# A two-layer megakernel: pair sums on TensorE with a 513th column, and a rearranged hand-over between its layers

## The chip, the cores and the metric

The kernel runs on one core of one Trainium2 chip. The metric is device time in microseconds (us), the median of several executions. Beside the timed executions there is one profiled execution, whose records make up the trace: which instruction ran when on which engine, and what it waited for. The engines are PE (TensorE matmul; PEld is its weight load), DVE (VectorE), ACT (ScalarE), POOL (GpSimd, which also issues the indirect DMAs) and SP (SyncE, which issues most other DMAs). PSUM is the memory that PE writes, in banks of 128x512 f32; SBUF is the working memory that all engines read.

## The reference

Eight sequences of 512 tokens with 128 channels go through two layers. In each the input x is layer-normed (xn), a mixer gives s, a mixture of experts gives g, and x becomes x + s * silu(g).

- Layer 0's mixer is a Mamba block (a recurrent scan over 16 states) with a small MLP; its experts are 24, of which each token uses two, in two rounds with a layer norm between them.
- Layer 1's mixer is causal attention with 8 heads over tokens scaled to unit length; its experts are 128, two per token.

What the change touches is, in the reference's words:

```python
# layer 0, per group of tokens; dispatch and combine pick two experts per token
h = moe_apply(xf, combine, dispatch, W1, b1)          # [tokens, 512], a weighted sum of two experts' rows
h = relu(layer_norm(h, lw, lb))
out = moe_apply(h, combine, dispatch, W2, b2)         # again a sum of two rows per token
g = silu(layer_norm(out + xn, ln_out_w, ln_out_b))
x = x + s * g
# layer 1
xn = (x - m) / sqrt(v + 1e-5)
l2 = sqrt(sum(xn * xn));  xa = xn / max(l2, 1e-12) * sqrt(128) * gamma    # attention's input
logits = xn @ wg                                                          # the router's input
```

## The kernel before

All of it is one program for one core. Python code lists the instructions; a planner then orders each engine's list by place in the program and an own model of costs, within the dependencies, so that an engine's order can differ from the program's (on DVE, a later pair's line 539 runs ahead of an earlier pair's line 553). On the chip each engine takes its list strictly in order and waits on semaphores. Tiles come from pools: a tag with `bufs=n` has n buffers, and the next use of a buffer waits for the last reader of the one before.

The scan of layer 0 (`model`, 64 steps of two states each) is cut into steps and dealt out beside the other work: 31 steps beside layer 0's experts, and the rest in the hand-over and beside layer 1's first six batches of attention. A step of `scan` takes, for each half of the channels, one multiply on DVE (line 655, 128x1024), two scans (657, 128x512), one multiply (658), and PE transposes that add the result up in PSUM (679). It holds `u`, a tile with four buffers, until 679 has read it.

The stages, with the tiles that matter:

- **First expert round** (`expert1`, 24 times). POOL gathers token rows, PE transposes and multiplies them with the expert's weights into `ph` (lines 503 and 504; tag "pe", four PSUM banks), ACT scales the result by each slot's routing weight into `hs` (505), and SP stores `hs` to `hs_dram`, rows of 512 floats (`store`, lines 474 and 475).
- **Hidden layer norm** (`between`, 16 pairs of token tiles). For each tile POOL gathers the two expert rows of 128 tokens into `hd` (128; four buffers, three pairs ahead). DVE adds the two rows and takes their sum along (539), which line 543 turns into minus the mean. ACT squares with that bias and sums (545), takes the root (549); DVE inverts it (550), applies mean and weight (553), then deviation and bias (554); SP stores to `hid_dram` (556). In four of the pairs `fold` also prepares attention weights on PE, from the same four banks.
- **Second expert round** (`expert2`), from `hid_dram` to `os_dram`.
- **Hand-over**, per batch of 512 tokens. `fetch` loads xn into `o` and gathers onto it, with adding DMAs, the two expert rows of each token (131, eight gathers). `after` layer-norms `o` on DVE (107 to 117) and makes the gate: weight, bias, SiLU, times s, plus x (595 to 599), the SiLU on ACT and the four others on POOL. `prepare` layer-norms the new x to `xn2`, transposes it, multiplies with the router's weights (811), picks the top two (816, 817), then takes the squares' sums on ACT (826), inverts their roots, scales and transposes to `xaT`, attention's input (836), and last calls `route`, which counts slots per expert on PE and DVE and scatters the token rows by POOL (880).
- **Attention beside the scan** (`early`, batches 0 to 5): per head, line 898 and 906 (scores), 908 (mask and maximum on DVE), 912 (exponential), 926 (transposes), 933 (values), 944 (sum). In each batch's heads the next batch is fetched (at head 1), gated (head 3) and prepared (head 4). PSUM for preparing, router and values is the scan's tag "pm" of two banks.
- **End**: attention of batches 6 and 7 beside layer 1's experts, and the final gathers (`finish`).

Of the kernel before, what the change touches and what calls it, by code (L numbers as in the profile page):

```python
# [47 lines left out]
def tile_kernel(ctx: ExitStack, tc: tile.TileContext, t: dict, out: bass.AP):  # L48
# [39 lines left out]
    hs_dram = dram.tile([E0 * SLOTS, DH], F32, name="hs_dram")  # L88
# [25 lines left out]
    def layernorm(pool, src, dst, n, eps, tag):  # L114
        mv, rs = norm_stats(pool, src, n, eps, tag)
        for j in range(n):
            V.tensor_scalar(dst[:, j, :], src[:, j, :], mv[:, j, 0:1], rs[:, j : j + 1], ALU.subtract, ALU.mult)

# [78 lines left out]
    zero = inv_pool.tile([P, L], F32, name="zero")  # L197
    G.memset(zero, 0.0)
# [8 lines left out]

    lg = mb.tile([P, NTT, E0], F32, name="lg", tag="yz")
# [281 lines left out]
    def expert1(e, w):  # L490

        we = w(e)
        px = ps_e.tile([P, SLOTS], F32, name="px", tag="pe")
        for c, r in enumerate(SROWS):
            xg = mg.tile([CP, D], F32, name="xg", bufs=8)
            gather(xg[:r], xn_dram, inv[:r, c, e : e + 1])
            T.transpose(px[:, c * CP : c * CP + r], xg[:r], ident[:r, :r])  # L497
        xT = mg.tile([P, SLOTS], F32, name="xTe", tag="xTe", bufs=2)
        S.copy(xT, px)
        hs = me.tile([CP, SG, DH], F32, name="hs", tag="big", bufs=4)  # L500
        for c, r in enumerate(SROWS):
            ph = ps_e.tile([CP, DH], F32, name="ph", tag="pe")
            T.matmul(ph[:r], chosen(e, r), bias[:, 0:DH], start=True, stop=False)
            T.matmul(ph[:r], xT[:, c * CP : c * CP + r], we, start=False, stop=True)  # L504
            S.activation(hs[:r, c, :], ph[:r], AF.Copy, scale=wsl[:r, c, e : e + 1])
        store(hs_dram, e, hs)

    def between():
# [6 lines left out]
        def begin(h, b0):  # L515
# [6 lines left out]
            hd = me.tile([P, n, 2, DH], F32, name="hd", tag="big", bufs=4)  # L522
# [7 lines left out]
        for i, (h, b0) in enumerate(pairs):  # L530
# [6 lines left out]
            var = st.tile([P, n], F32, name="lnh_v")  # L537
            for j in range(n):
                V.scalar_tensor_tensor(
                    hd[:, j, 0, :], hd[:, j, 0, :], 1.0, hd[:, j, 1, :], ALU.mult, ALU.add,  # L540
                    accum_out=mean[:, j : j + 1],
                )
            V.tensor_scalar(mean, mean, -1.0 / DH, None, ALU.mult)
            for j in range(n):
                S.activation(
                    hd[:, j, 1, :], hd[:, j, 0, :], AF.Square, bias=mean[:, j : j + 1],
                    accum_out=var[:, j : j + 1],
                )
            S.activation(var, var, AF.Sqrt, bias=eps6, scale=1.0 / DH)
            V.reciprocal(var, var)  # L550
            for j in range(n):
                x = hd[:, j, 0, :]
                V.scalar_tensor_tensor(x, x, mean[:, j : j + 1], lw, ALU.add, ALU.mult)
# [23 lines left out]
    def fetch(b):  # L577
# [7 lines left out]
        for h in range(H0):  # L585
            g = h * B + b
            gather_add(o[:, h, :], os_dram, row[:, g, 0:1])
        for h in range(H0):
            gather_add(o[:, h, :], os_dram, row[:, h * B + b, 1:2])
        return o, sb, xb  # L590

    def after(b, o, sb, xb):

        layernorm(st, o, o, NJ, eps6, "lno")
        G.tensor_tensor(o, o, bc(lno_w.unsqueeze(1), (P, NJ, D)), ALU.mult)
        G.tensor_tensor(o, o, bc(lno_b.unsqueeze(1), (P, NJ, D)), ALU.add)
        S.activation(o, o, AF.Silu)
        G.tensor_tensor(o, o, sb, ALU.mult)
        G.tensor_tensor(xb, o, xb, ALU.add)
        Q.dma_start(rows(x1_dram[b][:, :]), xb)  # L600
        return xb
# [190 lines left out]
    class Attention:  # L792


        def __init__(self, at, m_qk, w_vo, ps_x, ps_q, ps_s, ps_t, ps_o):
            self.at, self.m_qk, self.w_vo = at, m_qk, w_vo
            self.ps_x, self.ps_q, self.ps_s, self.ps_t, self.ps_o = ps_x, ps_q, ps_s, ps_t, ps_o

        def prepare(self, b, xb):
# [3 lines left out]
            layernorm(st, xb, xn2, NJ, eps5, "ln1")  # L803
# [18 lines left out]

            sq = at.tile([P, NJ, D], F32, name="sq2", bufs=1)
            ss = st.tile([P, NJ], F32, name="ss2")
            for j in range(NJ):
                S.activation(sq[:, j, :], xn2[:, j, :], AF.Square, accum_out=ss[:, j : j + 1])
            V.tensor_scalar(ss, ss, 1e-24, None, ALU.max)
            S.activation(ss, ss, AF.Sqrt)
            V.reciprocal(ss, ss)
            V.tensor_scalar(ss, ss, float(D) ** 0.5, None, ALU.mult)  # L830
            V.tensor_tensor(sq, xn2, bc(ss.unsqueeze(2), (P, NJ, D)), ALU.mult)
            pt = ps_x.tile([P, L], F32, name="pt3", tag=px)
            for j in range(NJ):
                T.transpose(pt[:, j * P : (j + 1) * P], sq[:, j, :], ident)
            xaT = at.tile([P, L], F32, name="xaT", bufs=3)
            S.activation(xaT, pt, AF.Copy, scale=gamma)
            self.route(b, xn2)
            return xaT
# [302 lines left out]
    def early():  # L1141
        for b in range(EARLY):
            for hd, _ in enumerate(beside.heads(b, ready[b])):
                if hd == 1:
                    got = fetch(b + 1)
                if hd == 3:
                    xb = after(b + 1, *got)
                if hd == 4:
                    ready[b + 1] = beside.prepare(b + 1, xb)
                yield  # L1150
# [28 lines left out]
    for b in range(EARLY + 1, B):  # L1179
        ready[b] = last.prepare(b, after(b, *fetch(b)))  # L1180
    weights2()
# [92 lines left out]
```

## Time and profile before

| | us |
|---|---|
| median of the 3 timed runs | 1579.48 (1574.91 to 1584.55) |
| the profiled execution, its own time | 1590.3 |
| its span (first to last record) | 1588.6 |
| busy: PE / DVE / ACT / POOL | 1213.1 / 1246.7 / 978.7 / 601.3 |
| mean granted TensorE clock | 0.896 |

The page's second part cuts the span into 40 slices of 39.7 us; a digit is the busy share in tenths. "PEclk" is the clock that the throttle granted to PE, in tenths of full speed; the last line is what the DMA engines moved.

```profile
PE   6878798213479888447878989989889798899863
DVE  5687667788846857869999999999899996465454
POOL 1166652656155433673412560042250402010465
PEclk9689999566689999867989999999999999999987
GB/s 181 183 225 261 253 216 253 234 244 245 117 219 226 218 188 154 145 60 107 62 85 68 93 114 48 58 103 73 61 68 61 92 35 14 143 108 235 62 101 96
```

The dip of PE at the seventh to tenth slice is the hidden layer norm, the dip at the seventeenth and eighteenth the hand-over; from there to the 33rd DVE is at 9.

How the views are read: a group of instructions shows its count, its busy time, the mean duration in ns, and the time its engine stood idle just before it with what ended that. The chain of waits is followed back from the last instruction to what released each step. A stretch's row gives the busy time of each engine in it.

### The profile page before, as it was taken

The numbers are of one execution on the slowest core, as the hardware profiler recorded it, in microseconds if no ns is written. First come the engines' busy times: TensorE is split into PE (matmuls) and PEld (weight loads), VectorE is DVE, ScalarE is ACT, GpSimd is POOL, SyncE is SP. The second block draws the span as 40 slices with busy tenths as digits, with TensorE's granted clock in tenths as the row PEclk, the third lists the DMA queues.
The fourth block names the chain that finished last, engine by engine and source line by source line (L and its number), as shares of the span: only waits on it lengthen the run. The fifth ranks groups of instructions, "written<-read, shape, count | busy, mean of one in ns | idle before, by whom it ended". The sixth has DMA issues, their size and how long they took to land.

```text
span 1588.6 us, 20612 instructions
## 1 busy us (share of the span) xinstructions
PE 1213.1 (76%) x6793; PEld 853.8 (54%) x6793; DVE 1246.7 (78%) x2783; ACT 978.7 (62%) x1728; POOL 601.3 (38%) x505
## 2 busy tenths in 40 slices
PE   6878798213479888447878989989889798899863
PEld 4534364113367777434556656766657576567542
DVE  5687667788846857869999999999899996465454
ACT  5356776575648677455767758667586674643442
POOL 1166652656155433673412560042250402010465
PEclk9689999566689999867989999999999999999987
DMA  6578767777377764523222341133121210538233
GB/s 181 183 225 261 253 216 253 234 244 245 117 219 226 218 188 154 145 60 107 62 85 68 93 114 48 58 103 73 61 68 61 92 35 14 143 108 235 62 101 96
DMA packets 170669, 218.84 MB, mean 138 GB/s; under 512 B 16618, under 2 KB 118074, under 8 KB 170562
## 3 DMA queue, kind: packets, MB, share of 16 engines
q1 hardware_dynamic: 126018, 99.39, 20.4%
q10 hardware_dynamic: 18432, 67.12, 13.0%
q0 software_dynamic: 26112, 51.01, 12.4%
q8 instruction: 54, 0.88, 0.2%
q14 instruction: 53, 0.43, 0.1%
HBM read 161.56 MB, written 55.84 MB: 137 GB/s over the span
## 4 chain that ended last, share of the span: by engine, by line
DVE 37%; PE 31%; DMA 8%; issue 8%; ACT 7%; POOL 6%; another core or an unknown queue 1%; SPq 1%; POOLq 0%; DVEq 0%; ACTq 0%
DVE u L657 10%; DVE u L658 4%; PE po L933 4%; PE sc L906 4%; DVE u L655 4%; DVE sc L908 3%; POOL o L131 3%; PE py L679 3%; PE pp L926 2%; PE po L573 2%; PE pc L611 2%; DVE s L944 2%; DMA hd<-hs_dram,row 2%; PE ph L504 2%; PE pv L891 1%
## 5 line engine op out<-in xcount | busy, mean ns | idle before, releaser
L657 DVE TENSOR_TENSOR_SCAN u<-da,u 128x512 f32<-128x512 f32 x256 | 312.6, 1243 | 64.1 <-ACT da L653 47.5
L679 PE MATMUL py<-ident,u 128*128 128x128 f32 x1024 | 164.3, 301 | 138.8 <-DVE u L658 137.3
L679 PEld LDWEIGHTS py<-ident,u 128*128 128x128 f32 x1024 | 131.8, 155 | 182.2 <-DVE u L658 162.6
L933 PE MATMUL po<-v,pT 128*128 128x129 f32 x1280 | 184.4, 287 | 37.3 <-DVE s L944 11.9
L933 PEld LDWEIGHTS po<-v,pT 128*128 128x128 f32 x1280 | 166.3, 198 | 67.8 <-issue 32.9
L653 ACT ACTIVATE da<-dt,a_neg 128x512 f32<-128x512 f32 x256 | 176.3, 719 | 35.6 <-DVE u L657 30.0
L912 ACT ACTIVATE prob<-sc,mn 128x128 f32<-128x128 f32 (+3 forms) x256 | 130.0, 527 | 106.2 <-DVE mn L908 65.0
L906 PE MATMUL sc<-xaT,qm 128*128 128x128 f32 (+3 forms) x512 | 177.9, 456 | 12.7 <-ACT prob L912 8.5
L655 DVE TENSOR_TENSOR u<-bb,lp 128x1024 f32<-128x1024 f32 x128 | 156.3, 1242 | 12.2 <-DMA bb<-xd_dram 12.0
L658 DVE TENSOR_TENSOR u<-u,cb 128x1024 f32<-128x1024 f32 x128 | 158.1, 1235 | 1.2
L908 DVE CUSTOM_DVE_ANT_0 sc<-sc,mask 128x128 f32<-128x128 f32 (+3 forms) x256 | 125.3, 501 | 35.9 <-PE sc L906 23.8
L131 POOL DMA_INDIRECT o<-os_dram,row x64 | 115.4, 1803 | 76.4 <-DMA cb<-xd_dram 31.2
L926 PE MATMUL pp<-ident,prob 128*128 128x128 f32 x640 | 112.3, 285 | 35.3 <-DVE pT L928 28.1
L880 POOL DMA_INDIRECT xs_dram<-xn,idx x64 | 76.2, 1191 | 160.5 <-DVE row L877 73.7
L926 PEld LDWEIGHTS pp<-ident,prob 128*128 128x128 f32 x640 | 79.8, 145 | 93.4 <-issue 33.8
L128 POOL DMA_INDIRECT hg<-hid_dram,inv x72 | 88.2, 1224 | 106.9 <-PE pht L568 76.6
L128 POOL DMA_INDIRECT xg<-xn_dram,inv x72 | 98.4, 1367 | 79.7 <-PE px L497 48.8
L906 PEld LDWEIGHTS sc<-xaT,qm 128*128 128x128 f32 x512 | 83.6, 197 | 56.3 <-ACT prob L912 23.4
L128 POOL DMA_INDIRECT hd<-hs_dram,row x64 | 80.2, 1254 | 70.2 <-DMA qkv_w<-in_qkv_w 23.5
L928 ACT COPY pT<-pp 128x384 f32<-128x384 f32 (+1 forms) x100 | 51.4, 514 | 62.5 <-PE pp L926 50.0
L573 PEld LDWEIGHTS po<-we,hgT 128*128 128x128 f32 (+1 forms) x576 | 71.7, 189 | 27.2 <-issue 21.4
L573 PE MATMUL po<-we,hgT 128*128 128x128 f32 (+1 forms) x576 | 80.6, 287 | 1.9 <-ACT hgT L570 1.8
(302 smaller groups left out, 2545.4 us busy)
## 6 DMA issues: line engine op xcount, KB each, us to landing
bb<-xd_dram ACTq DMA_DIRECT2D x64, 512.0 KB
cb<-xd_dram ACTq DMA_DIRECT2D x64, 512.0 KB
we<-in_W SPq DMA_DIRECT2D x48, 256.0 KB
hs_dram<-hs SPq DMA_DIRECT2D x24, 512.0 KB
hid_dram<-hd SPq DMA_DIRECT2D x32, 256.0 KB
we<-in_we SPq DMA_DIRECT2D x16, 512.0 KB
hs_dram<-hs SPq DMA_DIRECT2D x24, 192.0 KB
xb<-in_x SPq DMA_DIRECT2D x16, 256.0 KB
```

The source lines that it names most:

```text
L128: G.indirect_dma_start(dst, None, table[:, :], IOA(idx, 0))
L131: G.indirect_dma_start(dst, None, table[:, :], IOA(idx, 0), compute_op=ALU.add)
L573: T.matmul(po[:r, c, :], hT[:, f, :r], we[:, f, :], start=False, stop=(f == NJ - 1))
L653: S.activation(da[:, j, :], dt[:, hf, :], AF.Exp, scale=a_neg[:, hf, n0 + j : n0 + j + 1])
L655: V.tensor_tensor(u, bb, bc(dx[:, hf : hf + 1, :], (P, NC, L)), ALU.mult)
L657: V.tensor_tensor_scan(u[:, j, :], da[:, j, :], u[:, j, :], 0.0, ALU.mult, ALU.add)
L658: V.tensor_tensor(u, u, cb, ALU.mult)
L679: T.matmul(py[:, i, hf * P : (hf + 1) * P], us[hf][:, j, i * P : (i + 1) * P], ident, is_transpose=True, start=False, stop=(n0 + j == DS - ...
L906: T.matmul(sc[:, :w], qm[:, i * P : w], xaT[:, :w], start=True, stop=True)
L908: V.tensor_tensor_reduce(sc[:, :w], sc[:, :w], mask[:, L - w :], -1.0, FMAX, ALU.add, ALU.min, mn[:, i : i + 1])
L926: T.transpose(pp[:, c, :], prob[i][:, k * P : (k + 1) * P], ident)
L933: T.matmul(po[:, i - i0, :], pT[:, i * (i + 1) // 2 + k, :], v[:, k, hd % 4, :], start=(k == 0), stop=(k == i),)
```

## The change

Four parts, all in layer 0's end and the hand-over:

1. **Pair sums.** The rows of `hs_dram` get a 513th column: `expert1`'s scaling on ACT also sums what it writes and puts the sum there. `between` gathers rows of 513; DVE adds the two sums of a token (128x2 for a pair of tiles) and has the mean. The rows themselves are added by PE, as two products with the identity into one PSUM bank of tag "pe"; the square on ACT and the first apply on DVE read that bank.
2. **Batch 0's gate on DVE.** For batch 0 alone the second expert rows are gathered into a tile of their own (`o2`) without adding, DVE adds it, and the four gate operations run on DVE.
3. **Norms from the variance.** Attention's scale no longer comes from squares on ACT: the sum of squares of `xn2` is 128 times the variance times the squared inverse deviation, which three small DVE operations give.
4. **The router behind.** `prepare` makes `xaT` only; transposes for the router, its product, top two and `route` are a new function `choose`. For batch 0 it is called after the first head, for the others right behind `prepare`.

The tile `zero`, which fills a DRAM table near the start, moves to a pool that is closed earlier.

```diff
     xd_dram = [dram.tile([DTR + 2 * DS, L], F32, name=f"xd_dram{b}") for b in range(B)]
-    hs_dram = dram.tile([E0 * SLOTS, DH], F32, name="hs_dram")
+    hs_dram = dram.tile([E0 * SLOTS, DH + 1], F32, name="hs_dram")
     hid_dram = dram.tile([NTOK, DH], F32, name="hid_dram")
...
             V.tensor_scalar(dst[:, j, :], src[:, j, :], mv[:, j, 0:1], rs[:, j : j + 1], ALU.subtract, ALU.mult)
+        return mv, rs
...
     bias = inv_pool.tile([3 * 32, DH + D], BF16, name="bias")
-    zero = inv_pool.tile([P, L], F32, name="zero")
-    G.memset(zero, 0.0)
     pick = inv_pool.tile([3 * 32, E0], BF16, name="pick")
...
+    zero = rt.tile([P, L], F32, name="zero")
+    G.memset(zero, 0.0)
     lg = mb.tile([P, NTT, E0], F32, name="lg", tag="yz")
...
         S.copy(xT, px)
-        hs = me.tile([CP, SG, DH], F32, name="hs", tag="big", bufs=4)
+        hs = me.tile([CP, SG, DH + 1], F32, name="hs", tag="big", bufs=4)
         for c, r in enumerate(SROWS):
...
             T.matmul(ph[:r], xT[:, c * CP : c * CP + r], we, start=False, stop=True)
-            S.activation(hs[:r, c, :], ph[:r], AF.Copy, scale=wsl[:r, c, e : e + 1])
+            S.activation(
+                hs[:r, c, 0:DH], ph[:r], AF.Copy, scale=wsl[:r, c, e : e + 1], accum_out=hs[:r, c, DH : DH + 1]
+            )
         store(hs_dram, e, hs)
...
                 affine.append((lw, lb))
-            hd = me.tile([P, n, 2, DH], F32, name="hd", tag="big", bufs=4)
+            hd = me.tile([P, n, 2, DH + 1], F32, name="hd", tag="big", bufs=4)
             for j in range(n):
...
             var = st.tile([P, n], F32, name="lnh_v")
+            V.tensor_tensor(mean, hd[:, :, 0, DH], hd[:, :, 1, DH], ALU.add)
+            V.tensor_scalar(mean, mean, -1.0 / DH, None, ALU.mult)
+            sums = []
             for j in range(n):
-                V.scalar_tensor_tensor(
-                    hd[:, j, 0, :], hd[:, j, 0, :], 1.0, hd[:, j, 1, :], ALU.mult, ALU.add,
-                    accum_out=mean[:, j : j + 1],
-                )
-            V.tensor_scalar(mean, mean, -1.0 / DH, None, ALU.mult)
+                ph = ps_e.tile([P, DH], F32, name="phd", tag="pe")
+                for k in range(2):
+                    T.matmul(ph, ident, hd[:, j, k, 0:DH], start=(k == 0), stop=(k == 1))
+                sums.append(ph)
             for j in range(n):
                 S.activation(
-                    hd[:, j, 1, :], hd[:, j, 0, :], AF.Square, bias=mean[:, j : j + 1],
-                    accum_out=var[:, j : j + 1],
+                    hd[:, j, 1, 0:DH], sums[j], AF.Square, bias=mean[:, j : j + 1], accum_out=var[:, j : j + 1],
                 )
...
             for j in range(n):
-                x = hd[:, j, 0, :]
-                V.scalar_tensor_tensor(x, x, mean[:, j : j + 1], lw, ALU.add, ALU.mult)
+                x = hd[:, j, 0, 0:DH]
+                V.scalar_tensor_tensor(x, sums[j], mean[:, j : j + 1], lw, ALU.add, ALU.mult)
                 V.scalar_tensor_tensor(x, x, var[:, j : j + 1], lb, ALU.mult, ALU.add)
...
             gather_add(o[:, h, :], os_dram, row[:, g, 0:1])
+        o2 = af.tile([P, NJ, D], F32, name="o2") if b == 0 else None
         for h in range(H0):
-            gather_add(o[:, h, :], os_dram, row[:, h * B + b, 1:2])
-        return o, sb, xb
-
-    def after(b, o, sb, xb):
-
+            second = row[:, h * B + b, 1:2]
+            if b == 0:
+                gather(o2[:, h, :], os_dram, second)
+            else:
+                gather_add(o[:, h, :], os_dram, second)
+        return o, sb, xb, o2
+
+    def after(b, o, sb, xb, o2):
+
+        E = G
+        if o2 is not None:
+            E = V
+            V.tensor_tensor(o, o, o2, ALU.add)
         layernorm(st, o, o, NJ, eps6, "lno")
-        G.tensor_tensor(o, o, bc(lno_w.unsqueeze(1), (P, NJ, D)), ALU.mult)
-        G.tensor_tensor(o, o, bc(lno_b.unsqueeze(1), (P, NJ, D)), ALU.add)
+        E.tensor_tensor(o, o, bc(lno_w.unsqueeze(1), (P, NJ, D)), ALU.mult)
+        E.tensor_tensor(o, o, bc(lno_b.unsqueeze(1), (P, NJ, D)), ALU.add)
         S.activation(o, o, AF.Silu)
-        G.tensor_tensor(o, o, sb, ALU.mult)
-        G.tensor_tensor(xb, o, xb, ALU.add)
+        E.tensor_tensor(o, o, sb, ALU.mult)
+        E.tensor_tensor(xb, o, xb, ALU.add)
         Q.dma_start(rows(x1_dram[b][:, :]), xb)
...
             self.ps_x, self.ps_q, self.ps_s, self.ps_t, self.ps_o = ps_x, ps_q, ps_s, ps_t, ps_o
+            self.normed = {}
...
             xn2 = at.tile([P, NJ, D], F32, name="xn2", bufs=1)
-            layernorm(st, xb, xn2, NJ, eps5, "ln1")
+            mv, rs = layernorm(st, xb, xn2, NJ, eps5, "ln1")
+
+            sq = at.tile([P, NJ, D], F32, name="sq2", bufs=1)
+            ss = st.tile([P, NJ], F32, name="ss2")
+            V.tensor_tensor(ss, mv[:, :, 1], rs, ALU.mult)
+            V.tensor_tensor(ss, ss, rs, ALU.mult)
+            V.tensor_scalar(ss, ss, 1e-24 / D, None, ALU.max)
+            S.activation(ss, ss, AF.Sqrt)
+            V.reciprocal(ss, ss)
+            V.tensor_tensor(sq, xn2, bc(ss.unsqueeze(2), (P, NJ, D)), ALU.mult)
+            pt = ps_x.tile([P, L], F32, name="pt3", tag=px)
+            for j in range(NJ):
+                T.transpose(pt[:, j * P : (j + 1) * P], sq[:, j, :], ident)
+            xaT = at.tile([P, L], F32, name="xaT", bufs=3)
+            S.activation(xaT, pt, AF.Copy, scale=gamma)
+            self.normed[b] = xn2
+            return xaT
+
+        def choose(self, b):
+
+            at, (ps_x, px) = self.at, self.ps_x
+            xn2 = self.normed.pop(b)
             pt = ps_x.tile([P, L], F32, name="pt2", tag=px)
...
             V.tensor_reduce(se1[:, bs], lg, AX.X, ALU.add)
-
-            sq = at.tile([P, NJ, D], F32, name="sq2", bufs=1)
-            ss = st.tile([P, NJ], F32, name="ss2")
-            for j in range(NJ):
-                S.activation(sq[:, j, :], xn2[:, j, :], AF.Square, accum_out=ss[:, j : j + 1])
-            V.tensor_scalar(ss, ss, 1e-24, None, ALU.max)
-            S.activation(ss, ss, AF.Sqrt)
-            V.reciprocal(ss, ss)
-            V.tensor_scalar(ss, ss, float(D) ** 0.5, None, ALU.mult)
-            V.tensor_tensor(sq, xn2, bc(ss.unsqueeze(2), (P, NJ, D)), ALU.mult)
-            pt = ps_x.tile([P, L], F32, name="pt3", tag=px)
-            for j in range(NJ):
-                T.transpose(pt[:, j * P : (j + 1) * P], sq[:, j, :], ident)
-            xaT = at.tile([P, L], F32, name="xaT", bufs=3)
-            S.activation(xaT, pt, AF.Copy, scale=gamma)
             self.route(b, xn2)
-            return xaT
...
             for hd, _ in enumerate(beside.heads(b, ready[b])):
+                if hd == 0 and b == 0:
+                    beside.choose(0)
                 if hd == 1:
...
                     ready[b + 1] = beside.prepare(b + 1, xb)
+                    beside.choose(b + 1)
                 yield
...
         ready[b] = last.prepare(b, after(b, *fetch(b)))
+        last.choose(b)
     weights2()
...

```

## The prediction

> **What bounds the kernel now.** I read the stage table first (busy time of each engine in stretches of the span), cutting at three places where one engine waits for everything before it: GpSimd (POOL) gathers nothing of hs_dram until all 48 stores of it have landed (268 us), nothing of hid_dram until its stores have (423), nothing of os_dram until 646. At 730 the first attention head begins. Columns: stretch, length, busy us (and instructions) of PE, PEld, DVE, ACT, POOL; then granted TensorE clock, DMA share, GB/s.
>
> ```profile
> 97.00:268.00 171.00, 146.29 (x598) 79.73 (x596) 130.45 (x122) 120.98 (x200) 87.08 (x64) 0.96 0.75 242
> 268.00:423.00 155.00, 46.55 (x216) 35.36 (x216) 130.28 (x222) 101.04 (x180) 81.90 (x66) 0.64 0.69 219
> 423.00:646.00 223.00, 184.89 (x1332) 156.25 (x1332) 148.74 (x141) 149.03 (x284) 89.65 (x75) 0.94 0.64 197
> 646.00:730.00 84.00, 40.55 (x193) 30.51 (x194) 66.31 (x127) 37.39 (x70) 53.22 (x32) 0.67 0.41 101
> 730.00:1360.00 630.00, 558.79 (x3048) 388.31 (x3046) 584.72 (x1464) 431.91 (x748) 191.06 (x140) 0.96 0.24 69
> ```
>
> The second row is "between" (the hidden layer norm): DVE is busy 130 of 155 us and PE 47, at a clock of 0.64. The fourth is the transition: DVE idles 17.7 us of 84, and in the fifth row it is 93% busy. So DVE time counts in rows two and five, and DVE idle time in row four; in the first row PE leads with 86%.
>
> Then the groups, for prices, and the waits of DVE, first in 265 to 425 us, then in 640 to 730:
>
> ```profile
> L539 DVE SCALAR_TENSOR_TENSOR hd<-hd 128x512 f32<-128x512 f32 x32 | 21.6, 686 | 23.6 <-DMA hd<-hs_dram,row 14.1 <-issue 9.5
> L553 DVE SCALAR_TENSOR_TENSOR hd<-hd,lnh_m,lw 128x512 f32<-128x512 f32 x32 | 23.8, 775 | 0.4 <-ACT hd L545 0.4
> L128 POOL DMA_INDIRECT hd<-hs_dram,row x64 | 80.2, 1254 | 70.2 <-DMA qkv_w<-in_qkv_w 23.5 <-issue 14.9 <-ACT da L653 6.8
> ```
> ```profile
> DVE hd L539 <- DMA hd<-hs_dram,row: 14.1, 7, 3.3
> DVE hd L539 <- issue: 9.5, 4, 3.3
> ```
> ```profile
> DVE lno_st L107 <- DMA o<-os_dram,row: 12.6, 5, 7.1
> DVE ln_st L107 <- POOL xb L599: 4.5, 1, 4.5
> ```
>
> The 24.7 us in which DVE idles in "between" are nearly all before L539, the pair sum, waiting for gathered rows. In the transition DVE waits 12.6 us for gathered expert outputs and 4.5 us for POOL's gate.
>
> **The hidden layer norm.** Removed from DVE: 32 sums at 0.686 us, 21.6 us in all. Added: 16 column sums of 128x2, priced by L543 of the same shape (0.16 us), 2.6. Net 19.0 of DVE's 130. L553 reads PSUM instead of SBUF; a two-operand op with a per-partition scalar takes 344 ns from PSUM (L944) and 347 from SBUF (L711), so nothing. Squares on ACT from PSUM cost as in L612 (687 ns from PSUM) against L545 (713): nothing.
>
> Added to PE: 64 matmuls of 128x512 f32. The row is L504, two records to a matmul, and the timeline has it at both clocks:
>
> ```profile
> 126.72 1.91 PE L504 MATMUL ph<-we,xTe 128*128 128x512 f32 x2
> 257.72 1.02 PE L504 MATMUL ph<-we,xTe 128*128 128x512 f32 x2
> ```
>
> So 65 to 122 us more on a PE that is busy 47 of 155: 112 to 169. Which end? The stage rows give clock against busy share: 30% at 0.64, 48% at 0.67, 83% at 0.94, 86% at 0.96. PE now gets to some 75 to 80%, so I take 0.87: 64 x 1.02/0.87 = 75, the old 47 shrink to 47 x 0.64/0.87 = 34, together 109 us of a stage of about 140. PE fits, though it is in order, and a sum that waits for its gather holds the scan's transposes (L679) behind it, whose u buffers DVE needs.
>
> [...]
>
> What is the net 19.0 worth? Gathers set the rest: POOL issues 64 at 1.254 plus 0.30 us between two, 99 us, of the 126 that they take now (268.2 to 394.7), so POOL alone doesn't stop the stage from shrinking by 19. DMA moves 219 GB/s x 155 us = 34 MB; in 140 us that is 242 GB/s, what the first row sustains. But the chain of waits over 265 to 425 gives L539 only 5.6% of 160 = 9 us, and gathers, POOL and issue 40%. So 9 by the chain, 19 by the engine; I take 12, with 4 to 22 as ends: below 9 if PE's order costs something, above 19 if idle time before L539 goes too, now that PE does most of that waiting.
>
> **The 513th column.** Each hidden store (72 per kernel) now also reads ACT's accumulator. L545 does so: 186 ns per read, the next ACTIVATE starting 0.73 us after the one before; L653, without it, 0.61 to 0.66. So 0.07 to 0.19 us each, 5 to 13 us on an ACT that is busy 121 of 171. PE leads there, and the chain over 97 to 265 us has ACT hs with 4.6%: I charge 1 (0 to 6). Rows of 2052 bytes start at any multiple of four bytes; bytes grow 0.2%, and the trace has no gather of such rows. Lower bound 0; upper bound: gather landings, 17.9% of 160 = 29 us of the chain, half as long again, 14. I take 1, as no row moves more than a sliver of added data.
>
> [...]
>
> **The transition, batch 0.** Now: last rows land at 670.3; normalised o leaves DVE at 680.3; POOL reaches the gate only at 685.85, behind batch 1's gathers and zm (3.65 us), and ends it at 693.6. On DVE: four ops at 0.69 (L1045) and the SiLU (0.63), with three scan ops of 1.2 between, 7 us from 680.3 instead of 13.3: 6 earlier. Second rows gathered plainly cost POOL 0.95 to 1.25 instead of 1.56 to 1.8 each, 2 for four, less the extra add of 0.69. Then the first head: normed at 701.6, xaT at 721.5, first values at 729.6, because router work stood between, among it 8.7 us in which PE waited for zm (L751) to free a PSUM buffer. Without it: four small ops, multiply 0.68, transposes 1.1, copy 0.67, some 5 us; so the head can start about 20 us earlier. But the router's DVE work is only moved into the DVE-bound row, and five ops of 0.69 = 3.4 are new there. Worth is therefore DVE's idle time: 4.5 (POOL's xb) goes; of the 4.0 that batch 0's rows cost, half; of the 8.6 us that DVE stood before batch 1's rows (7.1 and 1.5), half, since other work is now ready but DVE is in order. 4.5 + 2 + 4.3 - 3.4 = 7. Ends 0 and 15.
>
> **Norms from the variance, router after xaT.** Per batch ACT loses four squares and four reads (2.0 us), DVE trades two small ops for three. In the 630 us row ACT is busy 69%; a prepared batch waits four heads for its turn. That slack hides it: 0 (4 faster to 2 slower); without the cover 2 us a batch. Moving `zero` changes no queue: its fill was issued at 43.5 us.
>
> **Sum.** -12 + 1 + 1 - 7 = -17. The profiled execution took 1590.3 us (span 1588.6), 10.8 above the median of the runs, 1579.5. So 1573.3 for such an execution, and 1562.5 as median; I say 1562.
>
> **Rivals.**
> - Gathers pace it: DVE waits as long as before for rows, now at the column sum, and the head start meets a full DVE. For it: 23.6 of 24.7 idle us are waits for rows. Against: POOL's 27 us of slack. Gain 4 + 2, less 2: 1575.
> - Both in full: 19 and 13, less 2: 1549. For it: POOL slack and DVE's 93% afterwards; against: the chain's 9.
> - PE becomes the bound: sums stay at the low clock, 47 + 122 = 169 us against 155, stage 14 longer; with 7 gained and 2 lost, 9 slower, 1589. It decides above (155 - 47)/64 = 1.7 us per sum, a clock under 0.6. For it: 0.64 now. Against: clock rises with busy share in every row.
> - The change does nothing where it matters, since the list order that the planner writes changes: any of these with another few us either way; in the ranges.
>
> **Numbers.** Forecast 0.52 (its own range 1554 to 1571), both in full 0.16, gathers 0.18, PE 0.14. A measurement here tells 0.5%, 8 us, from no change: below 1571.6 is faster, above 1587.4 slower. Faster: 0.52 + 0.16 + a quarter of the gathers' case = 0.73; slower: two thirds of PE's, 0.10; the same: 0.17. The range of 8 in 10 leaves out most of PE's case and the far end of the best: 1540 to 1584.
>
> **What would show it.** "Between" at some 143 us instead of 155 with DVE busy near 111 and PE above 100 at a clock over 0.8; no DVE wait for xb; first values near 708. Wrong if PE's records there take 0.9 us each, if DVE's wait for hd rows stays at 24 us, or if the first row grows by over 5 us.

## The result and the profile after

The changed kernel takes 1587.4 us (median of 12 runs) against 1581.1 for the kernel before in the same comparison: ratio 1.0048, 95% interval 1.0026 to 1.0071. It is half a per cent slower where 1.1% faster was predicted. A second comparison (after_again, below), on a chip on which the kernel before took 1551 us, gave 1.0063, 1.0040 to 1.0086.

The two profiled executions say the opposite, 1583.7 after against 1590.3 before: one execution lies below its median, the other above. Totals are therefore taken from medians, and profiles are read stage by stage.

The stage table after, cut at the same events as before (first gather of hidden rows, last hidden store, first gather of output rows, first attention values, end of the sixth batch, end); columns as above:

```profile
97.00:279.00 182.00, 146.55 (x597) 79.58 (x595) 131.80 (x123) 131.58 (x274) 74.33 (x64) 0.95 0.81 232
279.00:425.50 146.50, 108.09 (x342) 56.02 (x340) 107.48 (x170) 93.02 (x171) 75.48 (x66) 0.84 0.70 226
425.50:642.80 217.30, 182.43 (x1336) 153.75 (x1337) 151.24 (x143) 150.15 (x286) 97.83 (x75) 0.95 0.66 204
642.80:706.60 63.80, 31.55 (x175) 26.11 (x173) 58.91 (x96) 33.64 (x58) 47.07 (x26) 0.74 0.44 115
706.60:1339.10 632.50, 565.03 (x3020) 388.77 (x3020) 583.50 (x1498) 421.42 (x699) 186.76 (x141) 0.95 0.24 70
1339.10:1582.00 242.90, 182.92 (x1067) 129.93 (x1067) 126.29 (x431) 103.61 (x180) 72.86 (x76) 0.87 0.44 122
```

And the kernel before from its first attention values on, with the cuts moved to the same events:

```profile
729.60:1350.10 620.50, 550.29 (x3006) 383.03 (x3004) 584.08 (x1461) 427.29 (x742) 189.80 (x139) 0.96 0.25 70
1350.10:1588.60 238.50, 175.61 (x1067) 122.83 (x1067) 127.57 (x433) 101.85 (x183) 74.40 (x76) 0.91 0.45 124
```

Read top down: the first row grew from 171 to 182 us, at a DMA share of 0.81 instead of 0.75 that moves fewer GB/s. The second looks as forecast (146.5 us, PE 108 at a clock of 0.84, DVE 107); its sums, from the groups (64 products, two records to each):

```profile
L547 PE MATMUL phd<-hd,ident 128*128 128x512 f32 x128 | 65.1, 654 | 9.5 <-DMA hd<-hs_dram,row 4.9 <-issue 2.4 <-ACT lnh_v L553 1.4
```

The transition lost 18 us (82 to 64). Then the six batches beside the scan take 632.5 instead of 620.5 us **with the same DVE work**, 583.5 against 584.1 us: DVE idles 49 us there instead of 36. PE has 14 records more in this row (565 us instead of 550), as batch 0's router now stands in it.

DVE's waits after, first between the layers, then in 640 to 730 us:

```profile
DVE lnh_m L541 <- DMA hd<-hs_dram,row: 31.4, 7, 7.7
```
```profile
DVE o L606 <- DMA o<-os_dram,row: 3.7, 1, 3.7
DVE lno_st L107 <- DMA o<-os_dram,row: 3.5, 1, 3.5
```

The wait for hidden rows didn't stay at 24 us, it rose to 31. The waits of the transition went, POOL's gate among them.

### The profile page after: what moved, and what is told of

Same layout as the page of the kernel before. It is cut to its first block, busy times and chain, and to the rows that moved or that the text cites. A ratio compares the mean times of both kernels' runs of the same rounds, so it can differ in the third digit from the quotient of the medians.

```text
span 1582.0 us, 20905 instructions
## 1 busy us (share of the span) xinstructions
PE 1285.6 (81%) x6921; PEld 879.6 (56%) x6921; DVE 1220.3 (77%) x2741; ACT 975.9 (62%) x1741; POOL 580.6 (37%) x501
## 3 DMA queue, kind: packets, MB, share of 16 engines
q1 hardware_dynamic: 126018, 99.42, 20.8%
## 4 chain that ended last, share of the span: by engine, by line
DVE 37%; PE 27%; issue 11%; DMA 10%; ACT 8%; POOL 5%; another core or an unknown queue 1%; SPq 1%; ACTq 0%; DVEq 0%; POOLq 0%
DVE u L670 11%; DVE u L671 5%; DVE u L668 4%; PE po L952 4%; PE sc L925 4%; DVE sc L927 3%; PE py L692 2%; DVE s L963 2%; DMA cb<-xd_dram 2%; PE pp L945 2%; PE po L577 2%; DMA hd<-hs_dram,row 2%; PE ph L505 1%; POOL hd L129 1%; PE pc L624 1%
## 5 line engine op out<-in xcount | busy, mean ns | idle before, releaser
L692 PE MATMUL py<-ident,u 128*128 128x128 f32 x1024 | 160.9, 295 | 82.7 <-DVE u L671 79.8
L925 PE MATMUL sc<-xaT,qm 128*128 128x128 f32 (+3 forms) x512 | 185.9, 471 | 24.0 <-ACT prob L931 22.2
L952 PEld LDWEIGHTS po<-v,pT 128*128 128x128 f32 x1280 | 169.7, 201 | 60.3 <-issue 37.4
L692 PEld LDWEIGHTS py<-ident,u 128*128 128x128 f32 x1024 | 127.3, 151 | 130.5 <-DVE u L671 108.8
L927 DVE CUSTOM_DVE_ANT_0 sc<-sc,mask 128x128 f32<-128x128 f32 (+3 forms) x256 | 124.0, 494 | 39.1 <-PE sc L925 30.5
L132 POOL DMA_INDIRECT o<-os_dram,row x60 | 103.0, 1716 | 79.6 <-DMA cb<-xd_dram 30.9
L129 POOL DMA_INDIRECT hg<-hid_dram,inv x72 | 96.3, 1338 | 95.2 <-PE pht L572 66.7
L129 POOL DMA_INDIRECT xg<-xn_dram,inv x72 | 86.5, 1202 | 91.3 <-PE px L498 60.8
L129 POOL DMA_INDIRECT hd<-hs_dram,row x64 | 73.7, 1151 | 90.4 <-DMA we<-in_W 34.1
```

Source lines behind the costliest of these rows:

```text
L129: G.indirect_dma_start(dst, None, table[:, :], IOA(idx, 0))
L692: T.matmul(py[:, i, hf * P : (hf + 1) * P], us[hf][:, j, i * P : (i + 1) * P], ident, is_transpose=True, start=False, stop=(n0 + j == DS - ...
L925: T.matmul(sc[:, :w], qm[:, i * P : w], xaT[:, :w], start=True, stop=True)
L927: V.tensor_tensor_reduce(sc[:, :w], sc[:, :w], mask[:, L - w :], -1.0, FMAX, ALU.add, ALU.min, mn[:, i : i + 1])
L952: T.matmul(po[:, i - i0, :], pT[:, i * (i + 1) // 2 + k, :], v[:, k, hd % 4, :], start=(k == 0), stop=(k == i),)
```

## The experiments

Ratios are to the kernel before, with 95% intervals. The comparisons ran on different chips, on which the kernel before took 1551 to 1583 us; only ratios are compared across them. Theories go by the letters that the expectations give them.

### Is it the sums or the hand-over?

**sums_only** is the change without parts 2 to 4; **handover_only** is parts 2 to 4 on the kernel before. Both move `zero`.

> The sums on PE with their 513th column, and nothing else of the change. Theory A (the column spends what the sums bring): the stretch from 97 us to the first gather of a hidden row is 182 us as in the changed kernel instead of 171, the stretch between the layers some 146 instead of 155, the two nearly cancel, and the time is 0 to 4 us above the kernel before (ratio 1.000 to 1.003). Theory B (the loss is made in the hand-over and the attention heads): this part alone is 5 to 12 us faster (ratio 0.992 to 0.997). Theory C (the whole loss is here): 6 or more us slower.

> Batch 0's gate on DVE, the router behind its first head, the norm from the variance, `zero` moved; the sums stay on DVE and the rows at 512. Theory A (the loss is made by the 513th column): first attention values some 20 us after the last hidden rows earlier than before, of which 3 to 7 us are left at the end: ratio 0.995 to 0.998. Theory B (the loss is made here, since the heads are DVE-bound and DVE got five operations more): ratio 1.003 to 1.006. In either case the stretch up to the first gather of a hidden row stays at 171 us.

Measured: 1.0022 (0.9998 to 1.0046) and 1.0041 (1.0022 to 1.0060). The hand-over loses clear of the noise; the interval of the sums just takes in 1. In sums_only the first stretch is 180.7 us (theory A's 182), the hidden norm's 145.2. In handover_only the first stretch is 166.9 us, and first values come 62.1 us after the first output gather instead of 81.9, but the six batches take 637.8 us. So theory A holds for the sums, and theory B is right about where most is lost. Its reason, five more operations on DVE, is tested below.

### What the column costs

**reads_only**: accumulator reads alone. **wide_only**: 2052-byte rows alone. **sums_528**: sums_only with rows of 528 floats.

```diff
# reads_only
+        hsum = me.tile([CP, SG], F32, name="hsum", tag="hsum", bufs=4)
-            S.activation(hs[:r, c, :], ph[:r], AF.Copy, scale=wsl[:r, c, e : e + 1])
+            S.activation(hs[:r, c, :], ph[:r], AF.Copy, scale=..., accum_out=hsum[:r, c : c + 1])
# wide_only
+    hs_dram = dram.tile([E0 * SLOTS, DH + 1], ...)    # hs and hd as wide
+        S.copy(hs[:, :, DH], wsl[:CP, :, e])
# sums_528, from sums_only
+    hs_dram = dram.tile([E0 * SLOTS, DH + 16], ...)   # hs and hd as wide
+        S.copy(hs[:, :, DH:], wsl[:, :, 0:16])
```

> The kernel before, but the hidden stores' ACTIVATE also sums into a scratch tile that nothing reads: ACT's 72 accumulator reads without the column. If the reads make the first stretch longer, it is 178 to 182 us instead of 171 and the time 5 to 11 us longer (ratio 1.003 to 1.007). If the 2052-byte rows do, it stays within 2 us of 171 and the time is the same within 0.15%.

> The kernel before with a row pitch of 2052 bytes: hidden rows are stored and gathered with a 513th element, which one ACT copy per expert fills (24 copies, some 0.2 us each) and which nothing reads; no accumulator reads, no sums on PE. If the rows make the first stretch longer, it is 178 to 182 us at a higher DMA share than 0.75 and the time 5 to 12 us longer (ratio 1.003 to 1.008); if the reads do, it stays within 3 us of 171 and the time the same within 0.25%.

> Sums on PE with the column (sums_only, ratio 1.0022), but rows of 528 floats, so that each starts on a multiple of 64 bytes instead of any multiple of 4; 3% more bytes, and one ACT copy per expert that fills the spare columns. If the start of the rows is what makes other transfers take longer in the first stretch (DMA share 0.81 instead of 0.75), the share falls back under 0.78 and the stretch from 181 to 176 to 179 us, which the accumulator reads keep above 169, and the ratio is 0.996 to 1.000. If row starts don't matter and the reads and bytes do, the stretch stays at 180 or more and the ratio is 1.001 to 1.005.

Measured: 1.0004 (0.9980 to 1.0027), 1.0028 (1.0007 to 1.0050), 1.0050 (1.0023 to 1.0077). The first stretch in the three, and in a kernel that leaves this stage as it was (gate_only, below); columns as in the stage table:

```profile
97.00:275.70 178.70, 147.27 (x597) 79.88 (x595) 129.85 (x121) 127.80 (x270) 79.87 (x64) 0.95 0.71 231
```
```profile
97.00:274.10 177.10, 148.89 (x599) 81.81 (x598) 130.75 (x123) 121.06 (x220) 84.05 (x64) 0.93 0.83 233
```
```profile
97.00:272.80 175.80, 147.51 (x595) 79.08 (x594) 129.62 (x122) 130.09 (x294) 79.24 (x64) 0.95 0.74 243
```
```profile
97.00:266.00 169.00, 144.60 (x593) 78.84 (x591) 128.86 (x121) 119.88 (x198) 85.69 (x63) 0.96 0.74 245
```

Without either edit the stretch was 164 to 171 us in all fourteen profiles; with the reads it was 179, with the rows 177, with both 179 to 182, with both and 2112-byte rows 176. How much of that the reads and the rows make themselves isn't shown, because in these kernels the planner also wrote other lists for the stretch (in reads_only, PE's list leaves that of the kernel before at 101 us). What the reads add is ACT work, 14.0 us (after, same stretch), and no DMA:

```profile
L506 ACT ACTIVATION_READ_ACCUMULATOR hs<-ph,wsl 128x1 f32 (+1 forms) x72 | 14.0, 194 | 0.0
```

The rows are easier to separate: reads_only and sums_only list the stretch alike on all four engines, and between them only the rows differ (and where in memory the sums go). The stretch takes 178.7 and 180.7 us, a difference within the spread of the fourteen, but the DMA share is 0.81 instead of 0.71. The row of sums_only:

```profile
97.00:277.70 180.70, 147.40 (x596) 79.51 (x595) 132.32 (x123) 131.94 (x275) 78.84 (x64) 0.94 0.81 234
```

The trace's packet records say how: a 2052-byte packet takes a median 85 ns where a 2048-byte one takes 84 (means 91 to 96 and 95 to 98), so the rows themselves are not dearer. The others are: the 4096-byte packets of that stretch took a mean of 193 to 206 ns in the fifteen kernels without such rows (205 in reads_only), 244 to 258 in the four with them (244 in sums_only), and 213 with 2112-byte rows. Their median is 159 or 160 ns everywhere; a part of them takes much longer (the slowest tenth some 317 ns or more in the kernel before, 480 or more in the changed one). Rows of 2112 bytes, each starting on a multiple of 64, thus cure most of it. No run tells the start of a row from its length.

What reaches the end differs. The reads' 10 us are given back: in reads_only the stretch up to the last hidden store is 144.0 us instead of some 152, and the kernel is no slower. In wide_only that store comes at 431.3 us, and in handover_only, on the same chip and with the lists of the kernel before up to there, at 416.2; by the first output gather 2 us of this are left (640.5 against 638.4). And sums_528, its DMA share mended, was not faster than sums_only and missed the range expected for it; its hidden stretch was 155.4 us. Why is open.

### What the sums are worth

**sums_act** has the sums on PE, rows of 512, and the means from one more ACT pass over PSUM. **no_sum** leaves the sums out: only the first expert's row goes on, so all that follows works on other values, with the same instructions.

```diff
# sums_act, from sums_only
+            for j in range(n):
+                S.activation(hd[:, j, 1, 0:DH], sums[j], AF.Copy, scale=-1.0 / DH, accum_out=mean[:, j : j + 1])
# no_sum
-            for j in range(n):
-                V.scalar_tensor_tensor(hd[:, j, 0, :], hd[:, j, 0, :], 1.0, hd[:, j, 1, :], ..., accum_out=...)
+            V.tensor_tensor(mean, hd[:, :, 0, 0], hd[:, :, 1, 0], ALU.add)
```

> Sums on PE without the column: rows of 512, and ACT takes the means from PSUM in one more pass of 32 ACTIVATEs at 0.69 to 0.87 us, 22 to 28 us more on an ACT that is busy 93 of 146 us between the layers in the changed kernel. If the column is what spends the sums' gain, the first stretch is 171 us again, between the layers 146 to 152 instead of 155, and the time is 3 to 8 us below the kernel before (ratio 0.995 to 0.998). If the sums bring nothing in themselves, since gathers pace the stretch, between the layers stays at 155 and the ratio is 0.999 to 1.002.

> The kernel before without the 32 sums of the hidden rows on DVE, and nothing in their place: the second expert's row is left out, and the mean is made from one element of each row. DVE loses 21.6 us between the layers, no engine gets more, rows and heads stay. If DVE paces that stretch, it falls from 152 to 130 to 142 us and the ratio is 0.987 to 0.994. If gathers and the turn of their four buffers pace it, it stays at 146 to 152 and the ratio is 0.996 to 1.001.

Measured: 0.9982 (0.9954 to 1.0009) and **1.0003 (0.9978 to 1.0028)**. Taking 21.6 us off DVE and putting nothing in their place is worth nothing that can be measured. The hidden stretch of no_sum, DVE's wait in it, and waits of POOL's gathers in it:

```profile
263.50:409.80 146.30, 47.60 (x208) 37.30 (x208) 106.64 (x170) 85.48 (x162) 80.19 (x66) 0.60 0.72 231
```
```profile
DVE lnh_m L538 <- DMA hd<-hs_dram,row: 36.8, 13, 6.8
```
```profile
POOL hd L128 <- DMA hid_dram<-hd: 15.5, 7, 3.6
...
POOL hd L128 <- DVE hd L550: 5.7, 1, 5.7
POOL hd L128 <- DVE hd L549: 5.4, 2, 3.3
```

DVE's busy time fell from some 130 to 107 us, and its wait for rows rose to 36.8. The stretch still takes 146 us, as with the sums on PE: gathers pace it, and behind them the turn of the four `hd` buffers, which a gather can enter only when an earlier pair's result has left them. Between the first and the last of these gathers POOL is idle for 45 us, as in the kernel before (47), though DVE has so much less to do. From the 17th gather on, POOL stands 1.5 to 5.7 us before nearly every fourth one, until a hidden store has landed or DVE has finished with an older pair. (That the buffers set the pace is read from these waits; no run has more of them.) sums_act is the same with 151.4 us:

```profile
266.80:418.20 151.40, 107.57 (x344) 59.12 (x344) 106.74 (x138) 110.77 (x235) 77.22 (x66) 0.81 0.69 224
```

Nor did the planner take the gain away behind the stretch: from 548 us on (by the kernel before) the lists of PE, DVE, ACT and POOL are, instruction by instruction, those of the kernel before in no_sum, sums_act, sums_only, reads_only and sums_528, and in wide_only from 563 us on. What may be left of a gain is small: no_sum's profile reaches the first output gather at 626.9 us, and six profiles with DVE's sums, from chips on which the kernel before is as fast, reach it at 629 to 634.

### Which part of the hand-over?

**gate_only** is part 2, **norm_only** part 3, **order_only** part 4 (with the old norm), each alone.

> Of the hand-over only batch 0's gate on DVE, its second rows gathered plainly (and `zero` moved); router and norm as in the kernel before. Theory D (the router of batch 0, put behind the first head, stands on POOL and DVE just ahead of the next batch's gathers and makes their rows late): the gate alone is harmless, DVE's wait for POOL in the transition goes, ratio 0.996 to 1.000. Theory E (DVE-bound heads can't take more DVE work): 5 operations of 0.69 us more, ratio 1.001 to 1.003.

> Of the hand-over only the norm from the variance, for all eight batches; the router stays ahead of the heads' input. ACT loses 32 squares and their reads, DVE trades two small operations for three. Theories D and E: 0.999 to 1.001. If the small DVE chain costs the heads more than ACT's squares did, over 1.002.

> Of the hand-over only the order: the heads' input before the router in each batch, and batch 0's router behind its first head; gate on POOL, norm from ACT's squares. Theory D: this part carries the loss, ratio 1.002 to 1.006, first values some 12 to 20 us earlier than before after the last hidden rows, and in the heads DVE waits some 10 us or more for batch 1's rows, its gate and its router's counts, which it didn't wait for before. Theory E: 0.997 to 1.000, the lead staying.

Measured: 1.0052 (1.0022 to 1.0082), 0.9986 (0.9958 to 1.0014), **1.0199 (1.0155 to 1.0244)**. The three add up to 2.4%; together they cost 0.4%. If work alone counted, they would add up. Theories D and E both missed gate_only and order_only. DVE's waits in the six batches, before, after, and in order_only:

```profile
DVE rsum L938 <- PE po L933: 10.5, 11, 2.3
DVE sc L908 <- PE sc L906: 8.6, 15, 1.8
...
DVE lno_st L107 <- DMA o<-os_dram,row: 0.6, 1, 0.6
```
```profile
DVE sc L927 <- PE sc L925: 17.0, 22, 2.2
DVE rsum L957 <- PE po L952: 8.9, 10, 2.0
DVE pT L947 <- PE pp L945: 4.0, 4, 1.6
DVE lno_st L107 <- DMA o<-os_dram,row: 3.5, 1, 3.5
```
```profile
DVE lno_st L107 <- DMA o<-os_dram,row: 19.2, 6, 7.0
DVE sc L915 <- PE sc L913: 16.3, 24, 2.0
...
DVE ln_st L107 <- POOL xb L599: 9.4, 3, 5.0
```

What differs is where the planner lists the next batches' work. On DVE's list the output norm (L107) of batches 1 to 7 stands behind this many attention heads:

| | places, in heads | ratio |
|---|---|---|
| as the program writes it (the three pinned kernels below) | 4, 12, 20, 28, 36, 44, 48 | 1.037, 1.054, 1.058 |
| before; sums_only, sums_act, no_sum, reads_only, wide_only, sums_528 | 0, 0, 3.5, 10, 16, 28, 38 | 1; 1.0022, 0.9982, 1.0003, 1.0004, 1.0028, 1.0050 |
| after, handover_only | 0, 0, 2, 22.5, 26.5, 27.5, 30 | 1.0048, 1.0041 |
| gate_only | 0, 0.5, 1.5, 11.5, 15.5, 24, 30 | 1.0052 |
| order_only | 0, 0, 9.5, 9.5, 23.5, 24, 28.5 | 1.0199 |
| norm_only, act_norm | 0, 0, 9, 15.5, 28, 30, 44.5 | 0.9986, 0.9971 |
| hand_c2 | 0, 0, 1, 9, 14, 15.5, 28.5 | 1.0328 |
| hand_now | 0, 0, 0.5, 2.5, 11.5, 28.5, 29.5 | 1.0155 |
| before_245 | 0, 0, 4, 9, 30.5, 31, 45.5 | 1.0054 |

(Two expectations below number the batches of these places wrongly; the table is right.) PE's 14 further records aren't needed for the loss: order_only has more of them than the changed kernel, gate_only fewer than the kernel before, and both lose.

### Place or work?

The **pinned** kernels add an ordering edge, which holds the norm at its place in the program. **hand_c2** and **hand_now** are handover_only with batch 0's router behind the third head and right behind its input. **before_245** moves three calls in the kernel before.

```diff
# before_pin, handover_pin, order_pin: in norm_stats, and at the s1 accumulation
+            if tag == "lno" and held[0] is not None:
+                follows(x, held[0])       # x: the bn_stats; held[0]: the last s1 operation written
# hand_c2
-                if hd == 0 and b == 0:
+                if hd == 2 and b == 0:
                     beside.choose(0)
# before_245: fetch, after, prepare
-                if hd == 1: ... if hd == 3: ... if hd == 4:
+                if hd == 2: ... if hd == 4: ... if hd == 5:
```

> The kernel before with one more ordering edge: the first DVE operation of a batch's output norm may not stand ahead of the last values of the head behind which the program writes it (head 4, 12, 20 and so on; the planner had put it at 0, 3.5, 10, 16, 28, 38 heads). No work is added. Batch 1's norm leaves the transition. Theory O (the planner's place for the next batch's norms sets how long DVE waits): ratio 0.994 to 1.000, since in this kernel only the transition's wait of 8.6 us before batch 1's rows can go. Theory W (place doesn't matter, work does): 0.998 to 1.002.

> Parts 2 to 4 (hand-over alone, ratio 1.0041) with that ordering edge. Theory O: DVE's waits for gathered rows and for POOL's gate (5.0 and 2.6 us in the heads) go, the lead of some 20 us at the first values is kept better, ratio 0.990 to 0.998. Theory W: 1.002 to 1.006, as without the edge.

> The router behind the heads' input alone (ratio 1.0199, DVE waiting 19.2 us for rows and 9.4 us for POOL's gate in the heads) with that ordering edge. Theory O: these waits fall under 5 us together and the ratio to 0.996 to 1.004. Theory W: it stays above 1.012.

> Parts 2 to 4 alone with batch 0's router behind its third head instead of its first (behind the fetch of batch 1, ahead of its gate). Same work. Theory L (the late router of batch 0 is what costs: it stands ahead of batch 1's gathers on POOL and of its norms on DVE): DVE's 5.0 us wait for batch 1's rows goes and the ratio is 0.994 to 1.000. Theory P (the planner's order for the whole row decides, whatever is moved): anywhere between 0.99 and 1.02, and not explained by batch 1 alone; DVE's idle time in the heads' row moves with the ratio while its busy time stays within 5 us. Theory W (the work added by gate and norms costs): 1.003 to 1.005, as without the move.

> Parts 2 to 4 alone, but batch 0's router right behind its input, as for all other batches. Same work. Theory L: the loss goes, first values 10 to 15 us earlier than in the kernel before, ratio 0.994 to 1.000. Theory P: as in hand_c2, no telling. Theory W: 1.003 to 1.005.

> The kernel before, no part of the change; only the heads behind which the program writes the next batch's fetch, gate and preparation are 2, 4 and 5 instead of 1, 3 and 4. No work is added or removed. Theory P: the planner's list changes as a whole (batch 3's norm from 16 heads to 30, say) and the time moves by more than 0.5%, either way. Theories L and W: within 0.3% of the kernel before.

Measured: before_pin 1.0370 (1.0335 to 1.0405), handover_pin 1.0536 (1.0494 to 1.0579), order_pin 1.0576 (1.0543 to 1.0609). Both theories as I had put them fell: the planner's early places are no harm, they are worth 3.7% to the kernel before. Then hand_c2 1.0328 (1.0291 to 1.0366), hand_now 1.0155 (1.0114 to 1.0197), before_245 1.0054 (1.0028 to 1.0080). So order outweighs work: the same operations cost 0.4, 1.6 or 3.3% by where one call stands (the last outside theory P's range too), and a kernel without any part of the change loses 0.5% by three moved calls. A moved call changes much of the list, so which place in it costs isn't shown. Theory L falls too, as the router's late place is neither the loss nor its cure. The row of the six batches in hand_c2, and DVE's waits there:

```profile
693.60:1372.60 679.00, 572.61 (x3020) 396.67 (x3020) 579.92 (x1488) 425.34 (x709) 177.26 (x141) 0.93 0.22 65
```
```profile
DVE lno_st L107 <- DMA o<-os_dram,row: 29.6, 12, 5.8
DVE sc L924 <- PE sc L922: 26.0, 37, 4.4
DVE rsum L954 <- PE po L949: 16.3, 16, 2.0
DVE ln_st L107 <- POOL xb L609: 9.4, 3, 4.1
```

DVE is busy 580 us, 4 less than before, and idle 99 instead of 36. Over all kernels here DVE's busy time in this row is 560 to 598 us; its idle time runs from 32 (act_norm) to 127 us (order_pin), and most of the ratio goes with it. The exception is hand_now: its row takes 619 us, and its transition 92 instead of 82.

### The changed kernel again, and the best version

**act_norm** is sums_act with norm_only. **after_again** is the changed kernel unedited.

> Sums on PE with means from ACT and rows of 512 (sums_act, ratio 0.9982) together with the norm from the variance (norm_only, 0.9986), nothing else of the change. If the two add up: 0.995 to 0.999. Theory P: the list of the heads' row is that of norm_only (sums_act left it as it was), so it should add up here.

> The changed kernel unedited. Ratio 1.003 to 1.007 as in the first comparison; the stretch up to the first hidden gather some 180 us again, first values some 64 us after the first gather of an output row instead of 82, and the six batches beside the scan 630 to 638 us long instead of 620.

Measured: **0.9971 (0.9946 to 0.9996)**, the fastest kernel of this study and slightly better than both given ones, and 1.0063 (1.0040 to 1.0086). act_norm is what its two parts multiply to (0.9968), and behind the hidden stretch it has norm_only's lists. Its six batches:

```profile
716.40:1326.20 609.80, 550.36 (x3007) 381.25 (x3006) 577.68 (x1465) 428.39 (x702) 189.26 (x140) 0.97 0.23 69
```

They take 610 us, DVE idle 32, though it begins later than the changed kernel. after_again against no_sum, which came from the same chip and takes as long as the kernel before; the six batches, then the end:

```profile
697.20:1327.90 630.70, 560.84 (x3020) 386.95 (x3020) 585.51 (x1498) 421.40 (x699) 189.58 (x141) 0.96 0.24 70
1327.90:1551.90 224.00, 174.54 (x1067) 121.96 (x1067) 127.50 (x431) 103.49 (x180) 73.25 (x76) 0.92 0.47 132
```
```profile
709.50:1326.10 616.60, 550.34 (x3006) 384.05 (x3004) 584.01 (x1461) 427.40 (x742) 188.88 (x139) 0.96 0.24 70
1326.10:1544.00 217.90, 173.23 (x1067) 121.54 (x1067) 127.67 (x433) 101.72 (x183) 73.58 (x76) 0.92 0.49 136
```

The ledger of these two profiles: 12.6 us later at the first hidden gather (276.1 against 263.5), 4.1 back by the first output gather, 20.8 back in the transition (61.8 against 82.6 us), 14.1 lost in the six batches, 6.1 lost at the end (DVE waits 30.5 us for final gathers in the last batch's stretch, against 22.2): 7.9 us slower in all. (Against the kernel before, the first two terms would differ a little, as no_sum's hidden stretch is some 6 us shorter.)

## Why the prediction was wrong

- **Sums, -12 (4 to 22): the step that failed first.** It took DVE's 19 us as partly on the path, since POOL issues for only 99 of 126 us. no_sum shows the whole 21.6 us to be worth 0 (within some 4 us of it either way). The 27 us in which POOL doesn't issue are no slack: in no_sum they are waits for a buffer, and a faster DVE only waits longer for rows. My rival "gathers pace it", at 0.18, was right here (its time, 1575, was not). The forecast signs (stretch 143, DVE 111, PE over 100 at a clock over 0.8) all came true beside it: a stretch can look as predicted while the time it frees was never on the path. That it fell from 152 to 146 us proves no gain either: reads_only, with the sums still on DVE, fell to 144, after a later start.
- **Prices of the sums: right in total, by luck in the parts.** They keep PE busy for 65 us (75 predicted) and PE's other work there for 43 (34), in all 108 (109); PE didn't become the bound.
- **Column, +1 and +1: mis-sized.** The first stretch grew by some 11 us, past the 5 that I had named as the sign of error; the ends (6 and 14) held. Rows alone reach the end with 0.28% (0.07 to 0.50), 4 us; the reads' share is given back. I looked for the rows' price in their own landings, and it shows in other transfers. I also priced both as if the planner kept the stretch's lists, which it didn't.
- **Hand-over, -7 (0 to 15): the step that failed most.** Its mechanics were right: first values at 706.6 us (708 predicted), no wait for xb, DVE's idle time in the transition 4.9 us instead of 17.7. But alone it costs 0.41%, 6.5 us. "Worth is DVE's idle time" took the row behind it as fixed, 93% full of DVE work that begins earlier and so ends earlier. The planner rewrote that row's list; DVE's idle time moved there, from 36 to 49 us, and the end grew too (by 4 us in the first pair of profiles). None of the four orders tried with parts 2 to 4 alone was faster than the kernel before.
- **Norms, 0: right**, 0.9986 with an interval around 1.
- **"Any of these with another few us either way"** was the sentence on the planner. It was the largest term: 0.5% for moved calls alone, up to 3.3%. (The two halves measured alone, 0.22% and 0.41%, add up to 0.63%; the whole measured 0.48% and 0.63%.) It deserved a range of its own, and I could have priced it only by an experiment.
- **The profile** that all was read from, 1590.3 us, is above all 12 runs of the first comparison; it reached the first output gather at 647.7 us, where the ten kernels with the same lists up to there reached it at 629 to 639.

Shown: the sums' worth, that order outweighs work in the heads, the rows' effect on other packets. Argued only: that the buffers' turn paces the hidden stretch, and that even spacing of the next batches' norms is what fills DVE's list best (act_norm's and before's places are the most even early ones, the pinned ones are even but late, and no run varies spacing alone). Open: what the reads alone and the new lists alone did to the first stretch, why rows of 2112 bytes brought nothing to the end, and what the hand-over would be worth under an order made for it.

## What to carry to other kernels

Before pricing work taken off an engine, drop that work in a trial and see whether the time moves at all; if its wait grows by what its work shrank, the gain was never there. Where a planner writes the lists, an edit can reorder everything behind it (those of the hand-over did, those of the sums left the heads alone), so compare the lists, and compare the change with a neutral move of calls, before crediting or blaming its work. Look for the price of odd rows in other transfers; here rows of 2112 bytes brought those from a mean of 244 ns to 213, though they didn't mend the total.

## What the runs showed of the hardware

- Packets of rows of 2052 bytes, which start on any multiple of 4, took a median 85 ns (2048 bytes: 84), while the 4096-byte packets beside them took a mean of 244 to 258 ns instead of 193 to 206; with the same lists, 244 (sums_only) instead of 205 (reads_only). With rows of 2112 bytes these took 213 (sums_528).
- Chips differ: the same kernel before had medians of 1580 and 1583 us on two chips, 1551 to 1552 on three. Most of it sits in the last batch's stretch, 113 to 120 us on the former and 94 to 95 on the latter, in kernels that list this part alike.
